# The last three products of a graph network: TensorE's order written out step by step

## The chip, the cores and the metric

The kernel runs on one core of one Trainium2 chip. The metric is the device time of one execution in microseconds (us). Engine names: PE is TensorE (PEld its weight loads), DVE is VectorE, ACT is ScalarE, POOL is GpSimd, SP is SyncE.

## The reference

Four graph layers work in turn on x (2708 x 128) with one adj (2708 x 2708, float32). Each layer's output is added to x and normalized over the 128 features.

```python
h0 = (d[:, None] * (adj + I) * d[None, :]) @ x @ W0.T + b0      # layer 0, d = degree ** -0.5
den = exp(leaky_relu(s_row[:, None] + s_col[None, :]))          # layer 1
h1 = adj @ ((den / (adj @ den)) @ (x @ W1))
xt = logmap0(proj(mobius_add(proj(mobius_matvec(W2, x)), bias)))  # layer 2: tanh, atanh and
h2 = proj(expmap0(relu(logmap0(proj(expmap0(adj @ xt))))))        # norms of each row
pos, neg = (adj > 0) @ x, (adj < 0) @ x                           # layer 3
h3 = concat(pos, neg) @ Wn + bn * diag(adj) + (adj @ x) @ We + be * diag(adj) + x
x = layernorm(x + h)                                              # after every layer
```

## The kernel before

Features lie on the 128 partitions, nodes along the free axis. The first half of the run (layer 0 and the attention of layer 1) is left as it is. The change is in `fast_rest` (L1713), which computes the last three products with adj, each one pass over all of adj from HBM:

- **a1** = adj @ u (the end of layer 1). Its weights are `u_sb`. Each block's result goes to `after_attention` (L1970): the residual, sums of squares on PE (`sg`, `st`), the layernorm's factor spread over the partitions (`pr`), x, then the products with layer 2's weights (`mx`). `hyperbolic` (L2024) then makes h, the weights of a2, in long chains of small DVE and ACT operations with `Ln`, `Sqrt` and `Tanh`.
- **a2** = adj @ h. Its follow-up is `after_hyperbolic` (L2115): three group sums into `su` (squares before and after the relu, and the mean), spreads `mean` and `pg`, the norm (`st_l2`, `pr_l2`), and the products `pp` that give `edge` and `node`, the weights of a3.
- **a3** = edge.T with adj, plus node.T with sign(adj) (the loop at L2185, with masks made by ACT at L2203), then `norm_even` (L1912) and the output.

The nodes of the output are cut into blocks: for a1 and a2 five of 512 columns and a thin one of 148, for a3 six of 452 or 448 (`EVEN`). A block sums over 21 full tiles of 128 rows of adj (a "row" below) and a packed product for the 20 rows left over (`packs`). Its adj columns are loaded in two pieces of 11 and 10 tiles by `pieces` (L2265) on SP's queue into three buffers (`cb_a` with two, `cb_b`), taken in rotation.

Most rows are fp32 matmuls, two passes on PE. In some ("sharp", by the lists `SHARP` and `BEGIN`) the row is split by `split_rows` (one ACT and two DVE operations) and multiplied as three fp32r matmuls (`sharp_products`, L1796), two of them into a second accumulator, the upper sums, that is added in the follow-up. Weights are split once by `split_weights`.

The kernel is traced as plain Python, and a scheduler orders each engine's instructions when it is built, by a cost model of its own and the order of tracing. An engine then runs its list strictly in that order. `queued(PE)` chains what is traced within it behind the last such instruction on PE. Before the change, the chain is used for the attention, and in the three products only for the first rows of a2's block 0, which `meanwhile` puts among the last follow-up of a1; everything else in them is ordered by the scheduler. The results stay in PSUM: two accumulators in turn (`acc3`, `acc4`), one for upper sums (`acc5`), and five scratch places that `scratch` (L1819) hands out.

Of the kernel before, what the change touches and what calls it, by code (L numbers as in the profile page):

```python
# [10 lines left out]
F32 = mybir.dt.float32  # L11
# [32 lines left out]
SHARP = {"a1": (2, 5, 8, 11, 14, 17, 20), "a2": (2, 5, 8, 11, 14, 17, 19), "a3": (2, 4, 5, 7, 8, 10, 12, 13, 15, 17, 19)}  # L44
BEGIN = {"a1": 2 * NT, "a2": 2 * NT, "a3": 2 * NT}
# [21 lines left out]
def kernel(  # L67
# [1645 lines left out]
    def fast_rest(u_sb, pieces, scratch_pool, blk):  # L1713
# [40 lines left out]
        def split_weights(name, w, ks, dst):  # L1754
# [4 lines left out]
            while at < len(ks):  # L1759
# [13 lines left out]
                for j in range(n):  # L1773
                    sharp[name, ks[at] + j] = [t[:, j, :] for t in tiles3]
                at += n
# [54 lines left out]
        begun = {}  # L1830

        def product(weights, b, name, upto=NT, fixed=False):


            w = width(b)
            if name not in begun:
                begun[name] = [psum.tile([P, BW], F32, tag=f"acc{3 + b % 2}", name=name), 0, None]
            acc, done, pc = begun[name]
            half = NF if b == NB - 1 else KH
            layer = name[:2]  # L1840
            for k in range(done, min(upto, NF)):
                i, t = divmod(k, half)
                if t == 0:
                    pc = pieces(bslice(b), w, i * KH, half)
                if (layer, k) in sharp and BEGIN[layer] <= b * NT + k and b < NB - 1:
                    if name not in upper_sums:
                        upper_sums[name] = upper_tile(f"{name}_u")
                    rows3 = split_rows(pc[:, t, :w], w, split_tile(f"{name}_s{k}"))
                    sharp_products(acc, upper_sums[name], w, sharp[layer, k], rows3)
                    continue  # L1850
                with queued(PE) if fixed else nullcontext():
                    nc.tensor.matmul(  # L1852
                        acc[:, :w],
                        lhsT=weights[:, k, :],
                        rhs=pc[:, t, :w],
                        start=(k == 0),
                        stop=False,
                        skip_group_check=True,
                    )
            if upto == NT:  # L1860
                nc.tensor.matmul(
                    acc[:, :w],
# [6 lines left out]
            begun[name] = [acc, upto, pc]  # L1869
            return acc  # L1870

        def meanwhile(b, n):

            if b == NB - 1:
                product(h, 0, "a2_0", n, True)
                return queued(PE)
            return nullcontext()
# [12 lines left out]
        def group_wide(name, r, b):  # L1890

            n = 32 * len(tiles(b))
            two, term = (blk.tile([P, P], BF16, tag=t, name=f"{t}_{name}")[:n, :] for t in ("two", "term"))
            three_terms(two, r, blk.tile([P, P], F32, tag="rest3", name=f"rest3_{name}")[:n, :], term)
            return group_spread(scratch(name), two, b)
# [9 lines left out]
        def norm_groups(q, s, b, out):  # L1905

            st = scratch(f"st_{q}{b}")
            group_sums(st, 0, square_block(s, b, f"sq_{q}{b}"), b, mean_w)
            pr = group_wide(f"pr_{q}{b}", group_roots(f"gr_{q}{b}", st, b), b)
            nc.vector.tensor_mul(out, s, pr[:, : width(b)])  # L1910

        def norm_even(q, s, b, out):  # L1912
# [4 lines left out]
            nc.scalar.activation(sq[:, :w], s, AF.Square)  # L1917
            st = scratch(f"st_{q}{b}")
            for i in range(4):
# [11 lines left out]
            three_terms(two, r, blk.tile([P, P], F32, tag="rest3", name=f"rest3_{q}{b}")[:, :gw], term)  # L1931
            pr = scratch(f"pr_{q}{b}")
            for i in range(4):
                nc.tensor.matmul(
                    pr[:, i * gw : (i + 1) * gw],
                    lhsT=sel[:, i : i + 1].to_broadcast([P, P]),
                    rhs=two,
# [5 lines left out]
        def atanh(name, z, n):  # L1943
# [8 lines left out]
            ser = small(name + "s", n)  # L1952
            nc.vector.tensor_scalar(ser, w, 1.0 / 19.0, None, op0=ALU.mult)
            for d in (17, 15, 13, 11, 9, 7, 5, 3):
                nc.vector.scalar_tensor_tensor(ser, ser, 1.0 / d, w, op0=ALU.add, op1=ALU.mult)
# [5 lines left out]
            return ser  # L1961
# [8 lines left out]
        def after_attention(b, acc):  # L1970
# [15 lines left out]
            nc.scalar.activation(asq[:, :w], s[:, :w], AF.Square)  # L1986
            if b == NB - 1:
                with meanwhile(b, 2):
                    st = feature_sums(asq, b, f"st1_{b}", mean_w[:, 0:1])
            else:  # L1990

                sg = scratch(f"sg{b}")
                group_sums(sg, 0, asq, b, mean_w)
                v4 = blk.tile([P, P], F32, tag="v4", name=f"v4_{b}")
                nc.vector.tensor_copy(v4, sg[:, :P])
                pr = group_wide(f"pr{b}", group_roots(f"gr{b}", sg, b), b)
                st = scratch(f"st1_{b}")
                nc.tensor.matmul(st[:, :4], lhsT=v4, rhs=ident[:, ::32], start=True, stop=True)
            nc.vector.tensor_copy(var[:, ta:tb], st[:, :n])
            nc.scalar.activation(rstd[:, ta:tb], st[:, :n], AF.Sqrt, bias=eps_c)  # L2000
            nc.vector.reciprocal(rstd[:, ta:tb], rstd[:, ta:tb])
            if b == NB - 1:
                with meanwhile(b, 4):
                    pr = spread(scratch(f"pr{b}"), rstd[:, ta:tb], b)
# [93 lines left out]
        for b in range(NB):  # L2098
# [7 lines left out]
            if b in spans:  # L2106
                hyperbolic(b, *spans[b])
# [222 lines left out]
```

## Time and profile before

| | |
|---|---|
| median of three runs (lowest, highest) | 848.9 us (848.29, 850.11) |
| profiled execution | 845.43 us |
| its span, first to last instruction | 843.6 us |
| PE busy | 798.9 us, 95% of the span |
| DVE, ACT, POOL busy | 611.1, 489.3, 193.9 us |
| HBM read | 176.68 MB, 215 GB/s over the span |

The profile is one execution. In its lines an instruction group is named by engine, source line (L1852 is line 1852), operation and output <- inputs, with its shape and count; in a timeline the first number is the start, the second the length in us, and a bracket holds the engine's idle time before it and who ended it. Ends of matmuls are modelled, so the distance between two starts says more than a length.

### The profile page before, as it was taken

How to read it: one execution, taken by the hardware profiler on the slowest of the kernel's cores; microseconds unless marked ns; L12 is line 12 of the kernel's file. 1: busy time of each engine (PE TensorE's matmuls, PEld its weight loads, DVE VectorE, ACT ScalarE, POOL GpSimd, SP SyncE). 2: the span in 40 equal slices, each digit the busy share in tenths (PEclk: the TensorE clock that was granted, in tenths of full speed). 3: DMA queues.
4: the chain of work that ended last, by engine and by line, in shares of the span. 5: the costliest groups of instructions: out<-in, count | busy, mean ns of one | idle time of the engine just before them, and what ended most of it. 6: DMA issues, size and time to landing. Idle time of an engine off the chain costs nothing.

```text
span 843.6 us, 10200 instructions
## 1 busy us (share of the span) xinstructions
PE 798.9 (95%) x3360; PEld 440.5 (52%) x3360; DVE 611.1 (72%) x1386; ACT 489.3 (58%) x872; POOL 193.9 (23%) x173
## 2 busy tenths in 40 slices
PE   4699999998999999999999999999999999999994
PEld 3245454544344454444544455564455765677773
DVE  4776645589689888889895367978799864366763
ACT  4855554214387787777774143677455674566661
POOL 5231000000488886676621000000000000000000
PEclk9889999999999999999999999999999999999997
DMA  9997559089489555445425868797866840856600
GB/s 341 353 382 273 141 69 335 26 314 379 147 282 384 172 163 185 133 131 166 135 96 180 309 215 306 232 323 265 289 234 197 290 172 10 305 175 237 223 28 16
DMA packets 94984, 181.69 MB, mean 215 GB/s; under 512 B 6272, under 2 KB 37396, under 8 KB 94584
## 3 DMA queue, kind: packets, MB, share of 16 engines
q1 hardware_dynamic: 85228, 142.62, 49.4%
q0 software_dynamic: 7680, 34.85, 12.9%
q10 hardware_dynamic: 2016, 3.49, 1.2%
q8 instruction: 29, 0.48, 0.2%
q14 instruction: 31, 0.25, 0.1%
HBM read 176.68 MB, written 4.28 MB: 215 GB/s over the span
## 4 chain that ended last, share of the span: by engine, by line
PE 82%; DVE 9%; DMA 5%; ACT 3%; issue 1%; ACTq 0%; DVEq 0%
PE a L1852 16%; PE uacc L1641 13%; PE num L1610 12%; PE a L909 11%; PE a L2221 8%; PE a L2208 6%; DMA A<-in_adjT_dram 4%; PE a_u L1800 4%; PE t L847 2%; PE a L1800 2%; DVE jk L1373 2%; PE pp L2156 1%; PE su L271 1%; PE list L1463 1%; PE xw L1044 1%
## 5 line engine op out<-in xcount | busy, mean ns | idle before, releaser
L1615 ACT ACTIVATE ln<-num,inval,occ_l 128x512 f32<-128x512 f32 x144 | 98.4, 726 | 46.0 <-DVE rows_g L1613 42.3
L1641 PE MATMUL uacc<-att,xw_g 128*128 128x512 f32 (+1 forms) x288 | 116.7, 542 | 0.3 <-PE num L1610 0.3
L909 PE MATMUL a<-A,q_b 128*128 128x512 f32 (+2 forms) x264 | 110.5, 568 | 5.2 <-DVE q_b L944 3.3
L1558 POOL DMA_INDIRECT rows_g<-in_adjT_dram,row_i x48 | 96.9, 2020 | 62.5 <-PE num L1610 29.7
L1610 PE MATMUL num<-rows_g,w_all 128*128 128x512 f32 (+1 forms) x252 | 104.9, 543 | 0.0
L1613 DVE COPY rows_g<-num 2x512 f32<-2x512 f32 x138 | 81.2, 612 | 11.4 <-PE num L1610 7.6
L1852 PE MATMUL a<-cb,q_b 128*128 128x512 f32 (+1 forms) x210 | 85.1, 537 | 0.0
L1852 PE MATMUL a<-cb,xw 128*128 128x512 f32 (+1 forms) x210 | 84.4, 535 | 0.0
L1641 PEld LDWEIGHTS uacc<-att,xw_g 128*128 128x128 f32 x288 | 54.5, 190 | 55.1 <-issue 46.4
L2203 ACT ACTIVATE mask<-cb 128x904 fp32r<-128x904 f32 (+3 forms) x66 | 60.5, 921 | 37.1 <-PE a L2208 34.7
L2208 PE MATMUL a<-mask,node 128*128 128x452 f32 (+1 forms) x252 | 77.9, 426 | 1.1 <-ACT node L2167 0.5
L1633 DVE TENSOR_TENSOR att<-att,ln 128x1354 f32<-128x1354 f32 x48 | 74.4, 1549 | 2.5 <-ACT ln L1629 2.5
L909 PEld LDWEIGHTS a<-A,q_b 128*128 128x128 f32 (+1 forms) x264 | 47.2, 197 | 55.0 <-issue 47.3
L2221 PE MATMUL a<-cb,edge 128*128 128x452 f32 (+1 forms) x164 | 72.8, 546 | 0.0
L1610 PEld LDWEIGHTS num<-rows_g,w_all 128*128 128x128 f32 x252 | 45.3, 190 | 44.5 <-issue 34.7
L1629 ACT ACTIVATE ln<-ln 128x1354 f32<-128x1354 f32 x48 | 64.1, 1336 | 0.9
L1200 ACT ACTIVATE xw<-A 128x2048 f32<-128x2048 f32 (+3 forms) x36 | 56.9, 1582 | 3.0 <-DMA A<-in_adjT_dram 2.0
L1568 POOL DMA_INDIRECT xw_g<-xw_d,xw_i x24 | 54.2, 2260 | 15.6 <-issue 15.0
L2208 PEld LDWEIGHTS a<-mask,node 128*128 128x128 f32 x252 | 46.2, 188 | 20.2 <-issue 15.0
L1599 DVE TENSOR_SCALAR att<-q_b,gj_l 128x1354 f32<-128x1354 f32 x48 | 44.4, 926 | 10.9 <-PE uacc L1641 10.9
L1852 PEld LDWEIGHTS a<-cb,q_b 128*128 128x128 f32 x210 | 36.1, 189 | 27.1 <-issue 22.7
L1227 DVE TENSOR_TENSOR ut<-ut,A 128x2048 f32<-128x2048 f32 (+3 forms) x24 | 43.7, 1820 | 8.5 <-DMA A<-in_adjT_dram 7.6
(542 smaller groups left out, 1207.9 us busy)
## 6 DMA issues: line engine op xcount, KB each, us to landing
cb<-in_adjT_dram SPq DMA_DIRECT2D x10, 2816.0 KB
A<-in_adjT_dram SPq DMA_DIRECT2D x25, 1024.0 KB
cb<-in_adjT_dram SPq DMA_DIRECT2D x10, 2560.0 KB
B<-in_adjT_dram SPq DMA_DIRECT2D x18, 1024.0 KB
cb<-in_adjT_dram SPq DMA_DIRECT2D x5, 2486.0 KB
cb<-in_adjT_dram SPq DMA_DIRECT2D x5, 2260.0 KB
cb<-in_adjT_dram SPq DMA_DIRECT2D x2, 1554.0 KB
cb<-in_adjT_dram SPq DMA_DIRECT2D x1, 2464.0 KB
```

The source lines that it names most:

```text
L909: nc.tensor.matmul(acc[c][:, :w], lhsT=z[:kw, k, :], rhs=t[:kw, i, :w], start=c not in begun, stop=(d == NB - 1 and k == NT - 1), skip_gro ...
L1558: got = nc.gpsimd.indirect_dma_start(out=gat[q], out_offset=None, in_=adj_h, in_offset=bass.IndirectOffsetOnAxis(ap=row_i[:, h, g : g + 1] ...
L1610: nc.tensor.matmul(num[:, : cb - ca], lhsT=w, rhs=gat[q][:, ca:cb], start=True, stop=True)
L1613: nc.vector.tensor_copy(gat[q + 1][0:2, ca:cb], num[0:2, : cb - ca])
L1615: nc.scalar.activation(ln_n[q][:, ca:cb], num[:, : cb - ca], AF.Ln, scale=occ_l[:, g : g + 1], bias=inval[:, g : g + 1],)
L1629: nc.scalar.activation(ln_n[q], ln_n[q], AF.Exp, scale=-1.0)
L1633: nc.vector.tensor_mul(att[q], att[q], ln_n[q])
L1641: nc.tensor.matmul(uacc[h][c][:, : cb - ca], lhsT=xw_g[:, g, :], rhs=att[q][:, ca:cb], start=(g == 0), stop=(g == GM - 1),)
L1852: nc.tensor.matmul(acc[:, :w], lhsT=weights[:, k, :], rhs=pc[:, t, :w], start=(k == 0), stop=False, skip_group_check=True,)
L2203: nc.scalar.activation(mask[:, : tb - ta, :w], pc[:, ta:tb, :w], AF.Sign)
L2208: nc.tensor.matmul(acc[:, :w], lhsT=node[:, k, j, :], rhs=mask[:, t - ta, :w], start=(t == 0 and i == 0 and j == 0 and b != 1), stop=False ...
L2221: nc.tensor.matmul(acc[:, :w], lhsT=edge[:, k, :], rhs=pc[:, t, :w], start=(k == 0 and b == 1), stop=False, skip_group_check=True,)
```

## The change

The order of PE in the three products is laid down at build time. `steps` and `last_steps` list every block's rows as steps with a length (`TURN`) and the tiles of weights that they need. `play` keeps a clock, takes the next usable step of the first two unfinished blocks, and begins the splits and masks of up to three steps (`AHEAD`) early. The follow-ups are now generators that yield a pause (`PAUSE`) wherever PE has to wait for other engines; `play` resumes them among the steps when the pause is over by its clock (`resume`, `follow`), and all that they issue on PE is in the pinned chain. ACT, DVE and the queues are still ordered by the scheduler.

With it change: the lists of sharp rows (a1 from block 1 on instead of 2, a2 five instead of seven a block, a3 from row 10 of block 1); the shares of `hyperbolic` (tiles 0-11, 12-15 and 16-21 behind blocks 2, 3 and 5, instead of 0-11, 12-19 and 20-21 behind 2, 4 and 5), so that blocks 0 and 1 of a2 begin with tiles 0 to 15 and wait for 16; a2's three sums, issued together, with the relu on ACT; a2's norm as a chain of its own (`normed_on`); in a3 the join with the upper sums, done before the last products; the very last norm, spread by fp32 products without the split into bf16 terms; and `pieces`, which takes the buffer that was released longest ago from a list.

```diff
--- before.py
+++ after.py
...
-SHARP = {"a1": (2, 5, 8, 11, 14, 17, 20), "a2": (2, 5, 8, 11, 14, 17, 19), "a3": (2, 4, 5, 7, 8, 10, 12, 13, 15, 17, 19)}
-BEGIN = {"a1": 2 * NT, "a2": 2 * NT, "a3": 2 * NT}
+SHARP = {"a1": (4, 6, 9, 11, 14, 16, 19), "a2": (4, 7, 10, 14, 18), "a3": (3, 5, 7, 9, 10, 12, 13, 15, 16, 18, 20)}
+BEGIN = {"a1": NT, "a2": 2 * NT, "a3": NT + 10}
+PAUSE = {
+    "sums": 4,
+    "back": 1.2,
+    "root": 1.5,
+    "terms": 5,
+    "terms2": 8,
+    "scale2": 2.5,
+    "scale": 1.6,
+    "small": 1.6,
+    "h": 3.0,
+    "u": 5.0,
+    "mean": 3.5,
+    "g": 10,
+    "sq2": 3.5,
+    "node": 1.5,
+}
+AHEAD = 3
+TURN = {"row": 0.89, "sharp": 0.67, "thin": 0.26, "pack": 0.25, "mask": 0.4}
...
-        def product(weights, b, name, upto=NT, fixed=False):
...
+        def spend(us):
+            clock["us"] += us
+        def resume(c):
+            clock["us"] = max(clock["us"], c[0])
+            with queued(PE):
+                pause = next(c[1], None)
+            c[2] += 1
+            if pause is None:
+                next(g for g in (fronts, backs, others) if c in g).remove(c)
+            else:
+                c[0] = clock["us"] + pause
+            while later:
+                follow(backs, later.pop())
+        def follow(chains, work, most=1):
+            while chains is fronts and len(fronts + backs) > most:
+                resume((backs or fronts)[0])
+            while backs if chains is backs else any(c[2] < 2 for c in fronts + backs):
+                resume(next(c for c in backs + fronts if chains is backs or c[2] < 2 or c is fronts[0]))
+            c = [clock["us"], work, 0]
+            chains.append(c)
+            resume(c)
...
+        def beside(work, us=0.0):
+            others.append([clock["us"] + us, work, 0])
...
+        def earliest():
+            return min(fronts[:1] + backs[:1] + others, key=lambda c: c[0], default=None)
...
+        def usable(step):
+            return all(n in ready for n in step["needs"])
...
+        def play(blocks):
+            while any(blocks):
+                live = [b for b in blocks if b][:2]
+                pick = next((b for b in live if usable(b[0])), None)
+                bound = next((b for b in live if b[0]["begun"] or b[0]["joined"]), None)
+                if pick is None and bound is None:
+                    resume(earliest())
+                    continue
+                if bound is None or bound is pick:
+                    near = (pick + (live[1] if pick is live[0] and len(live) > 1 else []))[:AHEAD]
+                else:
+                    pick, near = bound, bound[:1]
+                for step in near:
+                    if not usable(step):
+                        break
+                    if not step["begun"]:
+                        step["begun"] = True
+                        if step["early"]:
+                            step["early"]()
+                step = pick.pop(0)
+                with queued(PE):
+                    step["now"]()
+                spend(step["us"])
+                if step["then"]:
+                    step["then"]()
+                while earliest() and earliest()[0] <= clock["us"]:
+                    resume(earliest())
+        def steps(layer, weights, b, needs, then):
...
+                if i not in hold:
+                    hold[i] = pieces(bslice(b), w, i * half, half)
+                return hold[i][0][:, t, :w]
...
+            def left(k):
+                if k + 1 == NF or (k + 1) % half == 0:
+                    free.append(hold[k // half][1])
...
+            def split(k):
+                hold["rows"][k] = split_rows(piece(k), w, split_tile(f"{name}_s{k}"))
...
+            for k in range(NF):
+                fine = full and k in SHARP[layer] and BEGIN[layer] <= b * NT + k
...
+                        "needs": needs(k) + ([(layer, k)] if fine else []),
+                        "early": (lambda k=k: split(k)) if fine else None,
+                        "now": lambda k=k: step(k),
+                        "us": TURN["sharp" if fine else "row" if full else "thin"],
...
+                    "then": lambda: then(b, acc()),
...
+            yield 3.0
...
-            three_terms(two, r, blk.tile([P, P], F32, tag="rest3", name=f"rest3_{q}{b}")[:, :gw], term)
+            if b < NB - 1:
+                three_terms(two, r, blk.tile([P, P], F32, tag="rest3", name=f"rest3_{q}{b}")[:, :gw], term)
+            yield 4.5
             pr = scratch(f"pr_{q}{b}")
+            spend(0.55)
...
-                    lhsT=sel[:, i : i + 1].to_broadcast([P, P]),
-                    rhs=two,
+                    lhsT=(sel[:, i : i + 1] if b < NB - 1 else ident[:, 32 * i : 32 * i + 1]).to_broadcast([P, P]),
+                    rhs=two if b < NB - 1 else r,
...
+            yield PAUSE["sums"]
...
-                pr = group_wide(f"pr{b}", group_roots(f"gr{b}", sg, b), b)
+                two = in_terms(f"pr{b}", group_roots(f"gr{b}", sg, b), b)
+                yield PAUSE["back"]
                 st = scratch(f"st1_{b}")
                 nc.tensor.matmul(st[:, :4], lhsT=v4, rhs=ident[:, ::32], start=True, stop=True)
+                spend(0.25)
...
+            else:
+                yield PAUSE["terms"]
+                pr = group_wide(f"pr{b}", two, b)
             nc.vector.tensor_mul(x[:, cs], s[:, :w], pr[:, :w])
+            yield PAUSE["scale"]
...
+            if b in spans:
+                beside(hyperbolic(b, *spans[b]), 1.0)
...
-            arg = atanh(f"a{q}", z, n)
+            arg = T("arg")
+            yield PAUSE["small"]
+            yield from atanh(arg, f"a{q}", z, n)
+            yield PAUSE["small"]
...
-        spans = {2: (0, 12), 4: (12, 20), 5: (20, 22)}
+                if i % 4 == 3:
...
+                if t == NF:
+                    packs["a2"] = pack("h", h[:, NF, :])
+            yield PAUSE["h"]
+            ready.update(("h", t) for t in range(ta, tb))
+        spans = {2: (0, 12), 3: (12, 16), 5: (16, 22)}
...
+        def weights_next():
+            dst = held_weights(col, "xw", "h_split")
+            for k in SHARP["a2"]:
+                while ("h", k) not in ready:
+                    yield 1.0
+                split_weights("a2", h, [k], dst)
+                yield 1.5
...
-            done = product(u_sb, b, f"a1_{b}")
-            if not b:
-                split_weights("a1", u_sb, range(NF), held_weights(late, "ut", "u_split"))
-            after_attention(b, done)
-            if b in spans:
-                hyperbolic(b, *spans[b])
...
+        beside(weights_first(), 1.0)
+        beside(tails_first(), 12.0)
+        play(
+            [
+                steps(
...
+                    lambda k: [("tail", 0)] if k == NF else [],
+                    lambda b, acc: follow(fronts, after_attention(b, acc)),
...
-                )
-                nc.vector.tensor_add(acc[:, :w], acc[:, :w], part[:, :w])
+                src = blk.tile([P, BW], F32, tag="ob", name=f"part{b}")
+                nc.scalar.activation(src[:, :w], upper_sums[f"a2_{b}"][0][:, :w], AF.Copy, scale=1.0 + 1.0 / LOW)
+                nc.vector.tensor_add(src[:, :w], acc[:, :w], src[:, :w])
+            usq = square_block(src[:, :w], b, f"usq{b}")
+            nc.scalar.activation(s[:, :w], src[:, :w], AF.Relu)
+            rsq = square_block(s[:, :w], b, f"rsq{b}")
+            yield PAUSE["u"]
             su = scratch(f"su{b}")
-            group_sums(su, 0, square_block(acc[:, :w], b, f"usq{b}"), b, ones)
-            nc.vector.tensor_scalar(s[:, :w], acc[:, :w], 0.0, None, op0=ALU.max)
+            group_sums(su, 0, usq, b, ones)
             group_sums(su, 2 * P, s, b, mean_w)
...
+            group_sums(su, P, rsq, b, ones)
+            spend(1.3)
...
+            yield PAUSE["mean"]
+            pm = group_wide(f"mean{b}", two_m, b)
...
-            pg = group_wide(f"pg{b}", g, b)
+            two_g = in_terms(f"pg{b}", g, b)
+            yield PAUSE["g"]
+            pg = group_wide(f"pg{b}", two_g, b)
...
-            norm_groups("l2_", s[:, :w], b, x[:, cs])
+            later.append(normed_on(b, s, w, cs, ta, tb))
...
+            yield PAUSE["sq2"]
+            st = scratch(f"st_l2_{b}")
+            group_sums(st, 0, sq, b, mean_w)
+            spend(0.45)
+            two = in_terms(f"pr_l2_{b}", group_roots(f"gr_l2_{b}", st, b), b, ("yt", "junk", "v4"))
+            yield PAUSE["terms2"]
+            pr = group_wide(f"pr_l2_{b}", two, b)
+            nc.vector.tensor_mul(x[:, cs], s[:, :w], pr[:, :w])
...
+            yield PAUSE["scale2"]
...
-        for b in range(NB):
-            done = product(h, b, f"a2_{b}")
-            if not b:
-                split_weights("a2", h, range(NF), held_weights(col, "xw", "h_split"))
-            after_hyperbolic(b, done)
...
+            yield PAUSE["node"]
+            ready.update(("n", t) for t in range(ta, tb))
...
+        beside(weights_next())
+        play(
+            [
+                steps("a2", h, b, lambda k: [("h", k)], lambda b, acc: follow(fronts, after_hyperbolic(b, acc), 2))
+                for b in range(NB)
+            ]
...
+        def last_steps(b):
...
+            def gathered():
+                s = blk.tile([P, BW], F32, tag="s", name=f"s3_{b}")
+                if upper[1]:
+                    joined(s[:, :w], upper[0][:, :w], x[:, cs])
+                    nc.vector.tensor_add(s[:, :w], s[:, :w], x[:, cs])
+                else:
+                    nc.vector.tensor_scalar(s[:, :w], x[:, cs], 2.0, None, op0=ALU.mult)
+                hold["s"] = s
...
+            def ending():
+                s = hold["s"]
+                nc.vector.tensor_add(s[:, :w], acc()[:, :w], s[:, :w])
+                ob = blk.tile([P, BW], F32, tag="ob", name=f"ob{b}")
+                yield from norm_even("l3_", s[:, :w], b, ob[:, :w])
+                nc.sync.dma_start(out=outT[:, cs], in_=ob[:, :w])
+            order = list(range(NF))
+            order[-2:] = order[:-3:-1]
+            for k in order:
...
+                        "needs": [("n", k)] + ([("n", k + 1)] if k % 2 else []) + ([("a3", k)] if fine else []),
+                        "early": lambda k=k, fine=fine: early(k, fine),
...
+                        "us": w / BW * (TURN["sharp" if fine else "row"] + 0.46),
...
+                        "joined": k in (NF - 2, *range(2, NF - 1, 2)),
...
-            nc.vector.scalar_tensor_tensor(s[:, :w], x[:, cs], 2.0, acc[:, :w], op0=ALU.mult, op1=ALU.add)
-            if upper[1]:
-                joined(s[:, :w], upper[0][:, :w], s[:, :w])
...
+        beside(weights_last())
+        play([last_steps(b) for b in range(NB)])
+        while earliest():
+            resume(earliest())
...
-                pool = cb_b if n % 3 == 2 else cb_a
+                place = free.pop(0)
+                pool, tag = place
                 nt = min(n_max, NF - k0)
-                t = pool.tile([P, n_max, BW if n_max == KH else w], F32, tag="cb", name=f"cb{n}")
+                t = pool.tile([P, n_max, BW if n_max == KH else w], F32, tag=tag, name=f"cb{n}")
...
+                return t, place
+            free = [(cb_a, "cb0"), (cb_a, "cb1"), (cb_b, "cb")]
```

## The prediction

> **What bounds the kernel now.** I read the page's busy table first, then its chain, then the busy time of each engine over the stretches of the three products that the change touches, and last TensorE's own timeline for its waits.
>
> ```profile
> span 843.6 us, 10200 instructions
> ...
> PE 798.9 (95%) x3360; PEld 440.5 (52%) x3360; DVE 611.1 (72%) x1386; ACT 489.3 (58%) x872; POOL 193.9 (23%) x173
> ...
> PE 82%; DVE 9%; DMA 5%; ACT 3%; issue 1%; ACTq 0%; DVEq 0%
> ```
>
> TensorE (PE) carries the end. The next answer's columns are length, then busy time and count of PE, weight loads, DVE, ACT and POOL, granted clock, DMA share and GB/s; its four stretches are the product a1, a2, a3, and the ending.
>
> ```profile
> 451.20:557.80 106.60, 103.67 (x390) 56.61 (x388) 70.58 (x210) 44.33 (x120) 2.69 (x3) 1.00 0.76 259
> 557.80:669.60 111.80, 111.80 (x500) 60.54 (x500) 93.94 (x319) 68.45 (x139) 0.00 (x0) 1.00 0.74 255
> 669.60:831.70 162.10, 160.97 (x713) 111.17 (x711) 96.98 (x204) 98.11 (x155) 0.69 (x4) 1.00 0.46 161
> 831.70:843.60 11.90, 1.00 (x12) 0.47 (x12) 3.83 (x8) 0.93 (x2) 0.00 (x0) 0.59 0.08 26
> ```
>
> PE idles 2.9 us of a1's 106.6, nothing in a2, 1.1 in a3, and nearly all of the 11.9 behind the last product. DVE is 84% busy in a2, so PE is little ahead of it there. DMA has room (0.46 to 0.76), and the order of buffers alone frees nothing. PE's waits:
>
> ```profile
> 480.28 0.80 PE L1861 MATMUL a<-tail,pack_u 128*128 128x512 f32 x1
> 482.52 0.42 PE L271 MATMUL sg<-asq,mean_w 128*32 128x128 f32 x8 [1.45 <-ACT asq L1986]
> 483.36 0.39 PE L1998 MATMUL st<-ident,v 128*128 128x4 f32 x2 [0.41 <-DVE v L1995]
> ...
> 534.45 0.43 PE L271 MATMUL sg<-asq,mean_w 128*32 128x128 f32 x8 [0.30 <-ACT asq L1986]
> 554.17 0.43 PE L271 MATMUL sg<-asq,mean_w 128*32 128x128 f32 x8 [0.25 <-ACT asq L1986]
> 711.94 0.93 PE L2208 MATMUL a<-mask,node 128*128 128x452 f32 x2 [0.53 <-ACT node L2167]
> 720.59 1.09 PE L2208 MATMUL a<-mask,node 128*128 128x452 f32 x4 [0.47 <-ACT mask L2203]
> ```
>
> At 480.28 block 0 of a1 ends; PE stands behind its follow-up though block 1's tiles are there. That is the wait the new order is able to fill. Behind the last product:
>
> ```profile
> 831.72 0.62 DVE L2247 SCALAR_TENSOR_TENSOR s<-x,a 128x448 f32<-128x448 f32 x1 [3.43 <-PE a L2238]
> 832.37 0.62 DVE L1815 SCALAR_TENSOR_TENSOR s<-a_u,s 128x448 f32<-128x448 f32 x1
> ...
> 835.43 0.22 DVE L286 CAST term_l<-gr_l 128x112 bf16<-128x112 f32 x1
> ...
> 836.70 0.56 PE L1934 MATMUL pr_l<-two_l,sel 128*128 128x112 bf16 x4 [2.59 <-DVE two_l L287]
> 837.29 0.62 DVE L1941 TENSOR_TENSOR ob<-s,pr_l 128x448 f32<-128x448 f32 x1 [0.65 <-PE pr_l L1934]
> ```
>
> **The change part by part.** The sum is against the profiled execution: span 843.6 us, 845.43 us in all. The median, 848.9, is 3.5 above it.
>
> *Waits removed.* The idle columns above sum to 3.41 us. They start at modelled ends, so they run short: from 480.28 to 482.52 is 2.24 us for a product that elsewhere holds PE 0.23, a loss of 2.0 where the column says 1.45. The new order puts block 0's sums at 4 us (PAUSE "sums") behind its end, among block 1's rows; the trace needed 2.24. Scaled by 2.0/1.45 the list is 4.7. I take -4.5, ends -3.4 and -6.
>
> *Sharp pieces.* The chain has 54 products of L1852 in 23.18 us, so a row of two is 0.86. From 600.03 to 602.45 PE does one sharp piece (three products of L1800) and two rows: 2.42 - 1.72 = 0.70. A sharp piece so saves 0.16 at 512 columns, and by the same count 0.15 at 452 (rows 0.76, three products at 0.203). a1 gets 28 for 21 (-1.1), a2 15 for 21 (+1.0), a3 51 for 44 (-1.1): -1.2 in all. Each adds 0.6 of ACT and 1.4 of DVE; seven more in a1 put 10 us on a DVE busy 71 of 107 us, where rows of PE hide it, and that cover is tested in the first rival. Ends 0 and -1.2.
>
> *a2's sums.* Today a block's three group sums into su interrupt PE up to three times (608.29, 609.52, 611.79). Each interruption makes the sums about 0.12 and the next row 0.20 longer than their undisturbed length. The change issues all three together: at most 2 x 0.32 x 5 blocks = 3.2 us, at least nothing. About half of the visits already touch other small work: -1.5.
>
> *The ending.* x is joined with the upper sums before the last product, so one DVE operation (0.65 with its gap) leaves the path. The four splits from 835.43 to 836.70 (1.27) go too, but four bf16 products, 0.59 to the next operation, become four fp32 ones of two passes. A pass of 128 columns takes 0.109 at the full clock (pr of the last a1 block); at 112 columns and half the clock, 0.19, so 8 x 0.19 + 0.3 = 1.8: +1.2. Net -0.65 - 1.27 + 1.2 = -0.7; ends -0.2 (products slower still) and -1.5 (full clock).
>
> *Moved and free.* The free list hands out the buffer released longest ago. Blocks 0 and 1 of a2 now share the three buffers, and a2_1's second half waits for a2_0's first. That is released about 12 us into a2, and its first use comes near 26; a 2.8 MB load at the 259 GB/s of this stretch takes 11 us. Cover 3 us; without it PE would stand for what is missing. SP issues the same loads in the same count, and the tail rows move behind 12 us of a1 with 4 us left before block 0 needs them (their landing is not shown; issue took 453.75 to 459.5). POOL moves only the padding memsets of the last block (its 0.69 us in a3's stretch are all it has there). Relu goes from DVE (0.69 a block) to ACT (0.6), which a2 leaves 39% idle. Free: 0.
>
> *The wait that the new order adds.* PE now does what comes next in the list, ready or not. Between a1 and a2 the last six tiles of h (16 to 21) come from one hyperbolic chain, where before two chains made eight and two. By the plan's own figures it is ready late: behind the last mx it counts 1.0, eleven pauses of 1.6 and 3.0, so 21.6 us, and its clock jumps some 5 us before tile 16. Only the plan's clock jumps; on the chip I set the chain against the products. PE from a1's end T: 32 rows of blocks 0 and 1 (27.5 us) and some 2.4 of follow-ups, so tile 16 at T+29.9. The chain: last mx behind 11 rows and other follow-ups, T+11.6; copies and squares 1.7; then 15.6 from first operation to first tile of h, as chain 4 took (564.77 to 580.34). T+29: about level. An ACT or DVE queue 10% slower costs 2 us. The table loads in that chain are these:
>
> ```profile
> 566.44 1.28 ACT L1949 ACT_TABLE_LOAD   x1
> 567.73 0.21 ACT L1949 ACTIVATE a4l<-a4l 128x8 f32<-128x8 f32 x1
> ```
>
> The trace charges 1.28 a load and no gap to the function behind it. The Trainium skill (ScalarE: Activation LUTs, What ACT_TABLE_LOAD costs) charges 1.28 and a drain of 1.38 for each switch. By that page five loads of a lone chain would, as an estimate, add 6.9 us, and PE would stand some 6 us; the sum goes by the row.
>
> The rest is a1's follow-ups: 1.6 us between pr and mx, of which DVE's multiply takes 0.68, and a split pair queued ahead takes 1.38: 0.5 over, in perhaps three of five blocks. So 1.5 there, 1 for the chain above: +2.5. Lower end 0 (the attention's pinned order left its L1641 group of 288 products 0.3 us idle); upper end: six of the 17 follow-ups lose what the first lost today (2.8 from 480.28 to 484), 17.
>
> Sum: -4.5 - 1.2 - 1.5 - 0.7 + 2.5 = -5.4, so 840.0 for such an execution and **843.5** for the median.
>
> **The rivals.** *Slower: DVE's queue holds PE at the follow-ups.* Splits start a block earlier in a1, and in the pinned order PE cannot pass a follow-up whose operand stands behind them. For: DVE 84% busy in a2, and the wait for st at 483.36 is DVE's. Against: the plan's pauses (4, 5, 3.5, 10, 8 us) are longer than the chains they cover, 2 to 4 us in the trace. Without new waits the gain is 7.9; above 9.6 us of them, about three and a half follow-ups at 2.8, the kernel is slower. Five give 14, so 855.
>
> *The waits only move.* What is filled after block 0 opens elsewhere, 4.5 lost again, and the joined sums save nothing: -1.2 - 0.7 leaves 847.0. For: a2 has no idle time to give. Against: the largest wait has one place and ready work beside it.
>
> *The hyperbolic chain is late.* 5 us more at tile 16, as the plan counts: 848. For: one chain of six tiles. Against: the chain timed above.
>
> **How the numbers follow.** A measurement tells about 0.2% (1.7 us) from no change. The forecast has 0.55, its own range 839 to 847; the slower rival 0.20; waits that move 0.17, on the edge between faster and same; the late chain 0.08, mostly same. Faster: 0.53 + 0.08 + 0.03 = 0.64; same: 0.02 + 0.09 + 0.04 = 0.15; slower: 0.21 with 0.01 of the chain. The low end takes every upper bound without new waits: -6 - 1.2 - 3.2 - 1.5 = -11.9, 837. The high end, 853, leaves out about a tenth, the worse half of the slower rival.
>
> **What would show it.** Right: no PE wait over 0.3 us between 480 and 484; a2's su products in one visit per block; from the last product's end to the end of the span about 11.2 us for 11.9; PE idle at tile 16 of a2_0 under 2 us. Wrong: PE idle before mx or pg with DVE as releaser; PE idle in a2 above 3 us; a cb load releasing PE.

## The result and the profile after

| | before | changed |
|---|---|---|
| median of the runs (lowest to highest) | 848.6 us (845.04 to 850.11) | 837.37 us (836.53 to 837.98) |
| profiled execution, its span | 845.43, 843.6 us | 836.53, 834.8 us |
| ratio, 95% interval | | 0.9873 (0.9841 to 0.9905) |

The kernel is 1.3% faster by these first runs; the forecast, 843.5 us, had the direction and about half the size, and its range (837 to 853) just holds the time. Ten later runs of the changed kernel (e4_after) gave 0.9899 (0.9866 to 0.9933).

The busy table and the chain of the changed kernel's page:

```profile
span 834.8 us, 10277 instructions
...
PE 796.1 (95%) x3372; PEld 444.4 (53%) x3372; DVE 619.8 (74%) x1400; ACT 498.5 (60%) x887; POOL 194.9 (23%) x173
...
PE 83%; DVE 8%; DMA 5%; ACT 2%; issue 1%; ACTq 0%; DVEq 0%
```

TensorE (PE) still carries the end, 2.8 us less busy. Busy time by stretch, with the prediction's columns; the stretches are again a1, a2, a3 and the ending:

```profile
450.40:553.30 102.90, 102.38 (x398) 58.18 (x396) 79.60 (x239) 49.30 (x125) 2.68 (x3) 1.00 0.78 266
553.30:665.90 112.60, 112.36 (x520) 60.87 (x520) 86.81 (x292) 67.27 (x143) 0.75 (x4) 1.00 0.75 262
665.90:823.40 157.50, 157.40 (x691) 112.19 (x690) 105.28 (x222) 103.80 (x161) 0.00 (x0) 1.00 0.47 162
823.40:834.80 11.40, 2.44 (x17) 1.94 (x16) 2.10 (x3) 0.93 (x2) 0.00 (x0) 0.61 0.09 28
```

PE's idle time in the three products has gone from 4.0 us to 0.9, of which 0.5 is the same start of a1 as before. At block 0's end, where PE stood twice, its timeline now reads:

```profile
470.27 0.80 PE L1958 MATMUL a<-tail,pack_u 128*128 128x512 f32 x1
470.91 3.60 PE L1952 MATMUL a<-cb,xw 128*128 128x512 f32 x8
473.94 1.03 PE L1820 MATMUL a_u<-a_s,u_split 128*128 128x512 f32 x2
474.81 0.40 PE L1820 MATMUL a<-a_s,u_split 128*128 128x512 f32 x1
475.13 0.43 PE L290 MATMUL sg<-asq,mean_w 128*32 128x128 f32 x8
```

Four rows and a sharp one of block 1 lie between the last product and the sums, 4.9 us later; no line has a bracket, so nothing waits.

**A measure that repeats.** Two profiles of the kernel before differ by 5.4 us ahead of a1, in code that the change leaves alone: the attention's last product ended between 450.4 and 460.9 us in the 14 profiles of this case. From there to the end of the span they agree closely. I call that the stretch and cut it at the starts of the products a1, a2, a3 and of the very last product. All in us:

| kernel | a1 | a2 | a3 | ending | stretch |
|---|---|---|---|---|---|
| before | 106.8 | 111.7 | 161.6 | 12.4 | 392.4 |
| before, again (e0_before) | 106.7 | 111.7 | 161.6 | 12.3 | 392.4 |
| changed | 102.9 | 112.6 | 157.0 | 11.9 | 384.4 |
| changed, again (e4_after) | 102.9 | 112.6 | 157.0 | 11.8 | 384.3 |
| e1_unpinned | 108.4 | 112.6 | 157.0 | 11.1 | 389.2 |
| e1b_free | 109.3 | 115.9 | 157.8 | 12.2 | 395.2 |
| e2_half_pause | 110.1 | 129.8 | 158.9 | 11.8 | 410.6 |
| e9_pin_first | 102.8 | 112.6 | 157.0 | 11.8 | 384.3 |
| e5_old_sharp | 103.9 | 116.6 | 157.5 | 11.7 | 389.7 |
| e6_sums_apart | 102.9 | 115.9 | 158.3 | 11.1 | 388.2 |
| e7_old_norm | 102.9 | 112.6 | 157.0 | 11.7 | 384.2 |
| e8_seven | 102.8 | 111.6 | 156.7 | 12.0 | 383.1 |
| e10_more | 110.2 | 112.7 | 156.2 | 11.5 | 390.6 |
| e3_rotate | 102.8 | 119.3 | 162.2 | 12.0 | 396.3 |

The change takes 8.0 us from the stretch. The profiled pair differs by 0.9 us more, which lies ahead of a1; that the rest of the 11.2 us between the medians lies there too is inferred, since those runs left no profile.

Do not read a2 and a3 apart: the cut between them moves against the follow-ups. In the kernel before, 12 of the 44 products of each of a2's three sums ran within a3, in the changed kernel 4. Taken together, a2 and a3 lost 3.6 us (unrounded) and a1 3.9.

### The profile page after: what moved, and what is told of

It is laid out like the page before. It is cut to its first block, busy times and chain, and to the rows that moved or that the text cites. A ratio compares the mean times of both kernels' runs of the same rounds, so it can differ in the third digit from the quotient of the medians.

```text
span 834.8 us, 10277 instructions
## 1 busy us (share of the span) xinstructions
PE 796.1 (95%) x3372; PEld 444.4 (53%) x3372; DVE 619.8 (74%) x1400; ACT 498.5 (60%) x887; POOL 194.9 (23%) x173
## 3 DMA queue, kind: packets, MB, share of 16 engines
q0 software_dynamic: 7680, 34.85, 13.1%
## 4 chain that ended last, share of the span: by engine, by line
PE 83%; DVE 8%; DMA 5%; ACT 2%; issue 1%; ACTq 0%; DVEq 0%
PE a L1952 17%; PE uacc L1660 13%; PE num L1629 12%; PE a L928 11%; PE a L2460 7%; PE a L2444 6%; PE a_u L1820 5%; DMA A<-in_adjT_dram 4%; PE a L1820 2%; PE t L866 2%; DVE jk L1392 2%; PE pp L2347 1%; PE su L290 1%; PE xw L1063 1%; PE mx L2136 0%
## 5 line engine op out<-in xcount | busy, mean ns | idle before, releaser
L2444 PE MATMUL a<-mask,node 128*128 128x452 f32 (+1 forms) x252 | 94.8, 458 | 0.0
L1632 DVE COPY rows_g<-num 2x512 f32<-2x512 f32 x138 | 81.2, 612 | 11.7 <-PE num L1629 7.6
L1952 PE MATMUL a<-cb,q_b 128*128 128x512 f32 (+1 forms) x222 | 89.5, 540 | 0.0
L2427 ACT ACTIVATE mask<-cb 128x904 fp32r<-128x904 f32 (+2 forms) x66 | 60.8, 923 | 35.0 <-PE a L2444 31.6
L1952 PE MATMUL a<-cb,xw 128*128 128x512 f32 (+1 forms) x196 | 79.4, 532 | 0.0
L2460 PE MATMUL a<-cb,edge 128*128 128x452 f32 (+1 forms) x150 | 68.9, 543 | 0.0
L1587 POOL DMA_INDIRECT xw_g<-xw_d,xw_i x24 | 54.2, 2259 | 15.9 <-issue 15.6
L1952 PEld LDWEIGHTS a<-cb,q_b 128*128 128x128 f32 x222 | 38.4, 190 | 31.5 <-issue 29.4
L1806 ACT ACTIVATE a_s<-cb 128x512 fp32r<-128x512 f32 x43 | 26.6, 626 | 40.3 <-PE a L1820 29.5
```

What stands on the lines that cost most here:

```text
L1632: nc.vector.tensor_copy(gat[q + 1][0:2, ca:cb], num[0:2, : cb - ca])
L1952: nc.tensor.matmul(acc()[:, :w], lhsT=weights[:, k, :], rhs=a, start=(k == 0), stop=False, skip_group_check=True)
L2427: nc.scalar.activation(mask[:, :n, :w], hold[i][0][:, t : t + n, :w], AF.Sign)
L2444: nc.tensor.matmul(acc()[:, :w], lhsT=node[:, k, j, :], rhs=mask, start=(k == 0 and j == 0 and b != 1), stop=False, skip_group_check=True,)
L2460: nc.tensor.matmul(acc()[:, :w], lhsT=edge[:, k, :], rhs=piece(k), start=(k == 0 and b == 1), stop=False, skip_group_check=True,)
```

## The experiments

My theory was that the order gains: follow-ups stand behind rows that are ready. The rivals were that counts gain (sharp rows, joined sums, ending), and that a pinned order is fragile.

### The two kernels again

> The kernel before, unchanged, measured as if it were an experiment. Theory: its waits at the first follow-up of a1 are a property of the order, so a second profile shows them again (about 2.2 us from the last product of block 0 to the sums), and PE spends 380 to 383 us from a1's first row to a3's last product. Rival: part of the 10.8 us between the kernels is an execution's own spread ahead of a1; then a1 begins 1 to 3 us later or earlier than at 451.2 us in this profile. Time: 846 to 850 us, ratio 0.998 to 1.002.

Measured: 846.0 us (843.55 to 850.88), ratio 0.9996 (0.9963 to 1.003); the stretch again 392.4, a1 beginning 5.4 us later than in the first profile. The wait is the order's, and the spread lies ahead of a1.

> The changed kernel once more, beside the next ones. The stretch from the attention's last product to the end is the same as in its first profile, 384.4 us within 0.6 (the ending has varied by as much with the clock of its last products). If the gain of the change is that stretch alone, 8.0 of 392.4, then the ratio over many runs is nearer 0.9905 than the 0.9873 of the first four, and the missing 2 to 3 us were the spread ahead of a1.

Measured: 840.8 us (836.65 to 845.27) against 849.81, ratio 0.9899; the stretch 384.3. By the two stretches alone the ratio would be 1 - 8.0/848 = 0.9906. The repeat agrees with that; the first comparison was 2.8 us lucky.

### The chain on PE taken away

```diff
-            with queued(PE):
+            with nullcontext():
                 pause = next(c[1], None)
...
-                with queued(PE):
+                with nullcontext():
                     step["now"]()
```

> The changed kernel with the steps and follow-ups still traced in the planned order, with the same pauses, but no longer chained on PE. Theory that the pin carries the order: the scheduler moves follow-ups back to where it would have them, and 2 to 5 us return: 839.5 to 842.5 us. Rival that the place in the trace carries it: within 1.5 us of the changed kernel's 837.4.

Measured: 843.08 us, ratio 0.9969 (0.9937 to 1.0002); the stretch 389.2, 4.8 more: a1 is 5.5 longer, and the ending 0.8 shorter for the clock (last section). PE's waits in a1:

```profile
483.23 0.43 PE L290 MATMUL sg<-asq,mean_w 128*32 128x128 f32 x8 [1.44 <-ACT asq L2102]
484.07 0.39 PE L2117 MATMUL st<-ident,v 128*128 128x4 f32 x2 [0.41 <-DVE v L2113]
485.59 0.50 PE L1820 MATMUL a_u<-a_s,u_split 128*128 128x512 f32 x1 [1.13 <-ACT a_s L1806]
486.51 1.08 PE L1820 MATMUL a_u<-a_s,u_split 128*128 128x512 f32 x2 [0.43 <-DVE a_s L1807]
```

The scheduler put block 0's last product behind eleven of block 1's rows (not fourteen, as the next expectation has it), as far back as in the kernel before, and nothing but the sums behind it: the waits of the kernel before. Everywhere else it kept the traced order. So the next kernel chains the first 40 us alone:

```diff
-            with queued(PE):
+            with queued(PE) if clock["us"] < 40 else nullcontext():
...
-                with queued(PE):
+                with queued(PE) if clock["us"] < 40 else nullcontext():
```

> The changed kernel with the chain on PE only for the first 40 us of the plan (blocks 0 and 1 of a1), the rest traced in the planned order but free. Without any chain the stretch was 389.2, all 5 us in a1, where the scheduler moved the last product of block 0 fourteen rows back. Theory that this one place is what the chain is worth: 384.4 to 385. Rival that the chain is worth something all over a1: 386 to 389.

Measured: one run, 840.99 us; the stretch 384.3. What the chain is worth, it is worth at blocks 0 and 1 of a1; behind them the place in the trace is enough.

### The order taken away

e1_unpinned, and the pauses (shown in part; all but "small" and "h") cut:

```diff
-    "sums": 4,
+    "sums": 0.1,
-    "terms": 5,
+    "terms": 0.1,
...
-    "g": 10,
+    "g": 0.1,
```

> The changed kernel without the chain on PE and with every pause of the three follow-ups cut to 0.1 us, so a follow-up is traced as one piece behind its block, as before the change, and the scheduler places it. Sharp rows, joined sums, the early join, the new ending and the list of buffers stay. Theory that order is what gains: the waits return, 4 to 7 us over the changed kernel, 841.5 to 844.5. Rival that counts and joined sums gain: 837 to 838.5, as changed.

Measured: 850.48 us, ratio 1.0052 (1.0015 to 1.0089), slower than the kernel before; the stretch 395.2. The order is worth 395.2 - 384.4 = 10.8 us to the changed kernel, and the rest of the change, without it, costs 2.8 over the kernel before. That the counts gain by themselves is out for the sum. I had expected 841.5 to 844.5; the order is worth about twice what I gave it.

The 10.8 us are not waits alone. a1 is 6.4 longer, with 4.0 us more of recorded idle time. a2 is 3.3 longer though PE never waits in it: the scheduler took the sums apart again (11 visits to `su`, 6 in the changed kernel), and one block more of `pp` falls into it. a3 is only 0.8 longer and keeps 3.8 us of its gain over the kernel before without the order.

### The pauses halved

```diff
-    "sums": 4,
+    "sums": 2,
-    "terms": 5,
+    "terms": 2.5,
...
-    "g": 10,
+    "g": 5,
```

> The changed kernel, pinned, with those pauses halved (the two of the last norm stay at 3.0 and 4.5). It measures how near the plan stands to my slower rival, in which PE stands at follow-ups that come too early. By the trace before, block sums need 2.2 us (now 2.0), the terms 3 (now 2.5), a2's squares 3.5 (now 2.5); the others have room. Theory that pauses carry slack about 2x: 3 to 9 us slower than the changed kernel, 840 to 846, with PE waits of 0.3 to 1.5 us at su and pr. Rival that the pinned order is fragile: over 12 us slower, behind the kernel before.

Measured: 865.33 us, ratio 1.0211 (1.0154 to 1.0267); the stretch 410.6, 26 more. Three of PE's waits (17 were over 0.15 us, the start of a1 aside; PE's idle time in the three products is 19.7 us more than in the changed kernel):

```profile
569.76 0.40 PE L312 MATMUL pr<-two_pr,sel 128*128 128x128 bf16 x4 [2.10 <-DVE two_pr L306]
576.36 0.69 PE L283 MATMUL pr<-ident,rstd 128*128 128x128 f32 x2 [2.11 <-DVE rstd L2121]
622.39 0.40 PE L312 MATMUL pg<-two_pg,sel 128*128 128x128 bf16 x4 [1.98 <-DVE two_pg L306]
```

Of the 17, 14 end with DVE and three with ACT. Ahead of `pg` at 622.39, DVE's list has a split (`a_s`) between the steps of the terms, and the split waits for ACT:

```profile
620.25 0.69 DVE L1807 TENSOR_TENSOR a_s<-a_s,cb 128x512 fp32r<-128x512 f32 x1 [0.83 <-ACT a_s L1806]
620.86 0.34 DVE L306 SCALAR_TENSOR_TENSOR rest_pg<-term_pg,behind,ug 128x128 f32<-128x128 bf16 x1
```

The first cast of the terms ended at 619.43; the next step began 1.4 us later. My expectation (3 to 9 us) fell to the rival: here this is the mechanism of my slower rival, and a plan whose pauses are half as long falls behind the kernel before. Not every wait is DVE's queue: ahead of 576.36, DVE itself stood 1.7 us for a square root of ACT's.

### The lists of sharp rows

```diff
-SHARP = {"a1": (4, 6, 9, 11, 14, 16, 19), "a2": (4, 7, 10, 14, 18), ...
-BEGIN = {"a1": NT, "a2": 2 * NT, "a3": NT + 10}
+SHARP = {"a1": (2, 5, 8, 11, 14, 17, 20), "a2": (2, 5, 8, 11, 14, 17, 19), ...
+BEGIN = {"a1": 2 * NT, "a2": 2 * NT, "a3": 2 * NT}
```

> The changed kernel with the lists of sharp rows from before. Read by the stretch from the attention's last product to the end of the span, which was 392.4 us in both profiles of the kernel before and 384.4 in the changed one. By my count of rows the old lists cost 1.2: a1 +1.1, a2 -1.0, a3 +1.1, so 385.6. Rival: the lists were chosen for where sharp rows fall (no first one at row 2, while the upper sums are still held), and old places make PE wait: 387 or more, with waits at the first sharp row of a block.

Measured: one run, 851.08 us beside 853.7 for the kernel before; the stretch 389.7, 5.3 more. a1 is +1.0, near the count's 1.1, and a3 +0.5. a2 is +4.0 though it has six sharp rows more. Its waits are not at a sharp row, as the rival had it, but at a1's last follow-ups:

```profile
563.36 1.92 PE L1952 MATMUL a<-cb,q_b 128*128 128x512 f32 x4
568.52 0.61 PE L312 MATMUL pr<-two_pr,sel 128*128 128x128 bf16 x4 [3.24 <-DVE two_pr L306]
576.39 0.43 PE L283 MATMUL pr<-ident,rstd 128*128 128x128 f32 x2 [0.33 <-DVE rstd L2121]
```

The same place in the changed kernel:

```profile
553.29 3.64 PE L1952 MATMUL a<-cb,q_b 128*128 128x512 f32 x8
557.17 0.40 PE L312 MATMUL pr<-two_pr,sel 128*128 128x128 bf16 x4 [0.24 <-DVE two_pr L306]
```

ACT's timeline ahead of the long wait: the square root that the terms need (`gr`, its sums begun at 561.35 and done at 561.8) stands behind the logarithm of a hyperbolic chain and two table loads.

```profile
562.11 1.28 ACT L2065 ACT_TABLE_LOAD   x1
563.41 0.20 ACT L2065 ACTIVATE a3l<-a3l 128x4 f32<-128x4 f32 x1
563.52 0.68 ACT L2230 ACTIVATE yt<-y,cb 128x128 f32<-128x128 f32 x2
564.22 1.28 ACT L2019 ACT_TABLE_LOAD   x1
565.51 0.37 ACT L2019 ACTIVATE gr<-sg,eps_c 128x128 f32<-128x128 f32 x1
```

In the changed kernel the same `gr` starts 2.9 us behind the start of its sums, here 4.2; from `gr` to `pr` both take 3.0. So ACT's order accounts for 1.3 of the 3.0 us that this wait is longer. The other 1.7 is the plan's own: PE had two rows (x4) to do between a1 and `pr`, where the changed kernel's plan put four (x8), 1.72 us more. A list of sharp rows can so cost by shifting which function ACT reaches first, and where the plan puts a follow-up. The next run bears on whether a1's list or a2's is the cause, but does not settle it: it has as many sharp rows in a2 as the old list, at other places.

```diff
-    "a2": (4, 7, 10, 14, 18)
+    "a2": (4, 6, 9, 11, 14, 16, 19)
```

> The changed kernel with seven sharp rows in each of a2's blocks 2 to 4 (rows 4, 6, 9, 11, 14, 16, 19), six sharp rows more. By PE's count a2 saves 1.0 us: the stretch 383.4. Theory that DVE is a2's second limit (87 of 112.6 us busy, 8.3 us more of splits here): PE waits appear at mean, pg or pr_l with DVE as releaser and the stretch is 385 or more. This also tells whether the wait of 3.2 us at the first pr in a2 under the old lists comes from splitting seven weights of h.

Measured: 840.34 us, ratio 0.9885 (0.9846 to 0.9925); the stretch 383.1, 1.2 less than the changed kernel beside it, and PE's only wait in a2 the same 0.25 us, which points to a1's list for the wait above. Six more sharp rows give what the count says (a2 is 1.0 shorter), and DVE is not a2's limit. In time it can't be told from the changed kernel (0.9899).

```diff
-BEGIN = {"a1": NT, "a2": 2 * NT, "a3": NT + 10}
+BEGIN = {"a1": 13, "a2": 2 * NT, "a3": NT}
```

(and the last norm as in e7_old_norm below)

> The changed kernel with sharp rows from row 13 of block 0 in a1 (three more) and from row 0 of block 1 in a3 (four more), and the last norm with bf16 terms. By count 3 x 0.16 + 4 x 0.15 = 1.1, and 0.2 at the end: 383.1 in the stretch, if DVE and ACT keep up (they are 77% and 48% busy in a1, 67% and 66% in a3). Rival: weights of u are not split in time at row 14 of block 0, and PE waits there: 385 or more.

Measured: 847.7 us, ratio 0.9969; the stretch 390.6. a3, with four sharp rows more, is 0.8 shorter. a1 is 7.3 longer, but not for late weights:

```profile
479.82 0.80 PE L1958 MATMUL a<-tail,pack_u 128*128 128x512 f32 x1 [5.80 <-DVE tail L1750]
```

The tail rows' two wide DVE operations ran from 475.19 here and from 463.83 in the changed kernel: the scheduler put them behind the new splits, and the pinned chain then held PE at block 0's last product.

### a2's sums apart

```diff
             group_sums(su, 0, usq, b, ones)
+            spend(0.43)
+            yield 0.5
             group_sums(su, 2 * P, s, b, mean_w)
+            spend(0.43)
+            yield 0.5
             group_sums(su, P, rsq, b, ones)
-            spend(1.3)
+            spend(0.44)
```

> The changed kernel with a2's three sums issued in three visits again, about one row apart, in the pinned order. My term for joining them was 1.5 us (0 to 3.2): the stretch goes from 384.4 to about 385.9, in a2 and the first third of a3, with no PE waits at su. Rival that a visit costs nothing beyond its own products: 384.4 to 384.7.

Measured: one run, 850.83 us beside 853.7; the stretch 388.2, 3.8 more (a2 +3.3, a3 +1.3, ending -0.8, the last for the clock). Two new waits, 0.68 and 0.74, are 1.4 of it:

```profile
624.63 0.43 PE L290 MATMUL st_l<-sq_l,mean_w 128*32 128x128 f32 x8 [0.68 <-ACT sq_l L2334]
733.36 0.93 PE L2448 MATMUL a<-mask,node 128*128 128x452 f32 x2 [0.74 <-ACT node L2363]
```

In a2 and a3, less those waits, 3.2 us belong to 13 more visits (19 for 6): 0.25 each, near the 0.32 of the prediction. The kernel before stood between: there the scheduler had joined some sums, and su was visited 13 times. So this run splits more than the change had joined, and its 3.8 us are not what joining gained. At 0.25 each, the seven visits from 13 to 6 make 1.7 us.

### The last norm as before

```diff
-            if b < NB - 1:
+            if b < NB:
                 three_terms(two, r, ...
-                    rhs=two if b < NB - 1 else r,
+                    rhs=two,
```

(and `sel` instead of `ident`)

> The changed kernel with the last norm as before: four splits on DVE and bf16 products in place of fp32 ones. From the last product's start to the end took 12.4 us before and 11.9 changed. The early join alone was to give 0.65; in the changed profile the fp32 products take 2.06 us to DVE's multiply where bf16 ones took 0.59 and the splits 1.27, so I expect 11.6 to 11.8 here: the swap gains nothing. Rival, that it gains 0.4 or more as fewer steps: 12.2 or more here.

Measured: one run, 842.38 us; the ending 11.7, the stretch 384.2. The swap to fp32 products gains nothing here, with the clock fallen ahead of them in both (last section); the early join is what shortened the ending: DVE's two wide operations behind the last product are one, 0.65 us less.

### The buffers in rotation

```diff
-                place = free.pop(0)
+                place = ((cb_a, "cb0"), (cb_a, "cb1"), (cb_b, "cb"))[n % 3]
```

> The changed kernel with its three adj buffers taken in rotation again. Only where two blocks run in turn does this differ: a2_2's first piece then waits for the last row of a2_0 (near 33 us into a2) instead of a2_1's first piece (near 27), is landed some 10 us later, and is needed near 40; a3_2's first likewise. Theory: 3 to 7 us more, with waits of PE or of its splits on a cb load at the start of block 2 in a2 and a3. Rival that loads have room anyway, as I priced the order of buffers at nothing for the kernel before: under 0.5 us.

Measured: one run, 851.77 us; the stretch 396.3, 11.9 more, at the two places named:

```profile
600.84 2.08 PE L1952 MATMUL a<-cb,q_b 128*128 128x512 f32 x2 [4.09 <-DMA cb<-in_adjT_dram]
...
738.41 0.68 PE L2444 MATMUL a<-mask,node 128*128 128x452 f32 x2 [3.50 <-ACT mask L2427]
```

The second wait is a load's too, through ACT, which makes the masks:

```profile
737.78 1.43 ACT L2427 ACTIVATE mask<-cb 128x452 fp32r<-128x452 f32 x2 [1.53 <-DMA cb<-in_adjT_dram]
```

The rotation gives a2_2's first piece the buffer that a2_0 still holds for its late tiles. Without the list of released buffers, the new order would lose more than it gains. The waits shown are 7.6 of the 11.9; where the other 4.3 lie I did not separate.

## Why the prediction was half right

*Waits removed, -4.5.* Right in place and about right in size: PE's waits at 482.52, 483.36, 534.45, 554.17, 711.94 and 720.59 are gone. a1 lost 3.9 us, of which its sharp rows are 1.0 (e5_old_sharp); 2.9 are left for its four waits, 2.4 by the idle column, 3.3 scaled as the prediction did. What the order is worth to the changed kernel is another quantity, 10.8 us (e1b_free). I read what the order of before lost; I did not see that the same scheduler would lose more with the new steps.

*Sharp rows, -1.2.* The price per row held in a1 (1.0 for 1.1) and a2 (1.0 for 1.0, e8_seven). In a3 it is less sure: four more rows gave 0.8 for 0.6, seven fewer in e5_old_sharp cost 0.5 for 1.1. That they could also move a wait (e5_old_sharp, 3.6 us of waits) was in no step.

*a2's sums, -1.5.* About right: seven visits fewer than before at the measured 0.25 make 1.7. The reason given, that about half of the visits already touch other small work, was not quite it: in three of the six blocks the sums were joined already, in part or whole, and 4 of the 13 visits touched other small work.

*The ending, -0.7.* Measured -0.5 to -0.6. The fp32 products took 2.06 us to DVE's multiply where I counted 1.8, and the swap of the norm came out at nothing, as worked out (a gain of 0.07 in the sum).

*Buffers, 0.* Right for the order of before, which waited on no load, and incomplete: the new order needs the list, by 11.9 us. The cover of 3 us that I named for a2_1's second half held; the piece that would have been late was the next, a2_2's first.

*The new wait, +2.5.* This is the term that failed: nearly nothing came of it. In the changed kernel PE waits 0.24 us at `pr` (557.17) and nowhere else over 0.2 in the three products, the start of a1 aside. Tile 16 of a2_0 was needed at T+29.8 (29.9 predicted), and h was there at T+27.6 (29 predicted): the chain took 13.1 us from first operation to first tile, where chain 4, sharing ACT and DVE with another, had taken 15.6. The Trainium skill (ScalarE: Activation LUTs, What ACT_TABLE_LOAD costs) adds 1.38 us of drain to each load; no load here shows one, 562.11 + 1.28 to 563.41 above leaves 0.02. The 1.5 us for mx behind a split pair did not come either.

So the sum without that term, -7.9, is the measured -8.0, and laid beside the two traces it is so by about the same terms: in a1 2.9 for the waits and 1.0 for sharp rows; in a2 and a3 together 3.6, where the waits are 1.0 to 1.4, the visits 1.7 and sharp rows, by count, next to nothing, with some 0.5 to 0.9 left open; 0.5 at the end. This is an account, not an experiment for each term. Taken out of the changed kernel one at a time, order, lists, sums and buffers cost 10.8, 5.3, 3.8 and 11.9, far more than 8.0 together: the parts depend on each other, and each removal breaks something besides. The rival with DVE's queue is real, and stands no more than a factor of two in the pauses away. The waits did not just move, and the hyperbolic chain was not late. The ratio of 0.9873 held a further 2.8 us that no step could give, since by the repeat they lie ahead of a1. That the first time came so near the low end of the range (837) is chance.

## What to carry to other kernels

Where an engine works through a fixed list, list its waits with the work that stands ready behind each: here a planned order took about what that list said. A planned place in the trace got nearly all of it, with a hard chain needed only where the scheduler put one product eleven rows late. Such an order carries pauses, buffers and counts with it: halving the pauses or keeping the old buffer rule made the kernel slower than it had been, so change these together and measure them apart. Compare profiles from a point where the unchanged part ends: two kernels 1 us apart could be told there, when whole runs spread over 8 us.

## What the runs showed that I had not expected

The unchanged part ahead of a1 varies by up to 10.5 us between profiles (attention's end at 450.4 to 460.9), while the stretch behind it repeated within 0.1 in the two kernels profiled twice; only its ending can vary by more. What varies ahead of a1 I did not look into.

The ending varies with PE's clock. In all 14 profiles the granted clock fell to half between 2.7 and 5.2 us behind the start of the last product. The changed kernel's fp32 spread falls inside that time; here the clock fell at 2.9 us, the spread began at 3.6:

```profile
826.59 2.02 PE L2050 MATMUL pr_l<-gr_l,ident 128*128 128x112 f32 x8 [1.45 <-DVE gr_l L2042]
```

and in e1_unpinned, where the clock was full for the first 0.8 us of it:

```profile
834.03 1.25 PE L2050 MATMUL pr_l<-gr_l,ident 128*128 128x112 f32 x8 [1.45 <-DVE gr_l L2042]
```

The ending was 11.9 us in the one and 11.1 in the other (11.1 also in e6_sums_apart, where the clock fell at 4.8 us). This bears on the swap of the last norm: with bf16 products DVE's last multiply began 5.4 us behind the start of the last product in e7_old_norm and 5.2 in e10_more, with fp32 ones 5.7 in the changed kernel and 4.8 to 4.9 in these two. The swap gains or loses a few tenths by where the clock falls. The Trainium skill (TensorE: Matmul & The Clock Gate, Seeing it yourself) shows one throttle event 5.2 us behind the last matmul; here that is the latest of the 14, and the earliest came at 2.7, both counted from the last large product, with small ones still behind it.
